# The skip term of a state-space scan written into the PSUM bank by ACT, the gate moved to DVE, and FFN weights binarised on ACT alone

## The chip, the cores and the metric

The kernel runs on one NeuronCore of a Trainium2 chip. A core has five engines that run side by side, each through its own list of instructions in order: PE (TensorE, matrix products), ACT (ScalarE, one input and a function), DVE (VectorE, element-wise work and scans), POOL (GpSimd, element-wise work) and SP (SyncE, which here only issues DMAs). They wait for each other through semaphores. The metric is the device time of one execution in microseconds (us); lower is better. All data is fp32.

## The reference

One layer of a network on x of shape 8 x 384 x 1024 (batch, channels, tokens). Its first half is a selective state-space model, its second half a feed-forward network (FFN) with binarised weights.

```python
t = layernorm(layernorm_over_channels(x))
xm, z = split(t @ in_proj_w.T)                  # 768 channels each
xc = silu(conv3(xm) + conv_b)
dt, Bm, Cm = split(xc @ x_proj_w.T)             # 24, 16, 16
dt = softplus(dt @ dt_proj_w.T + dt_proj_b)
dA  = exp(dt * A)                               # 16 states per channel
dBu = dt * xc * Bm
h_t = dA_t * h_{t-1} + dBu_t                    # along the 1024 tokens
y = (sum over states of h * Cm) + xc * D        # the skip term is xc * D
y = y * silu(z)                                 # the gate
x = x + gelu((y @ out_proj_w.T) @ mlp_w1.T + mlp_b1) @ mlp_w2.T + mlp_b2
...
# FFN, for each of 5 groups of rows of W1 (1536 x 384) and W2 (384 x 1536):
wg = W[g]; z = wg - wg.mean(); Wb[g] = z + (sign(z) - z)   # rows beyond 5 groups stay 0
y = x @ Wb.T + b; y = clip(y * 128 / (max|y| + eps), ...)
```

The FFN's quantisation works in 5 groups over the batch of 8, so that only the first five batch elements have an FFN output that is not zero.

## The kernel before

The work of each batch element b is cut into a front (`s1`: norms, input projection, convolution, dt), a scan (`s2`, `scan`, `scan_tile`), a back (`s3`: output projection and MLP) and, for b under 5, the FFN (`ffn`). Results pass between these parts through DRAM tensors. Once, at b = 0, `binarise` turns W1 and W2 into signs and stores them.

The scan of one batch element has 12 units. A unit (loop over m in `scan`) is one PSUM bank py of 128 x 512, the sum over states for its channels. It needs 8 scan tiles of 128 x 1024 (4 groups of states times 2 groups of channels). For each tile, `scan_tile` has ACT write da = Exp(dt * A) (L792), POOL write u = dtx * B (L797), DVE run the recurrence (L801), and then DVE (L818) or, for three of the eight, POOL (L815) multiply by C. After each four tiles PE adds the 16 results into py with 128 x 32 matmuls (L728); the first of them opens an accumulation group (`start=True`) and so overwrites the bank. Batch elements 0 and 7 are scanned as two halves of 512 tokens, with the state kept between them.

When a unit's sums are complete, xc and silu(z) for it are loaded into xr and zr. DVE computes xr = xr * D + py (L758), POOL multiplies xr by zr (L768, or L764 for the last batch element, straight into yg), and SP stores xr to the DRAM tensor yg_d (L774), from which the back loads it.

No order is written out by hand. `Plan.add` records each operation with an engine, a cost in microseconds and the tiles that it reads and writes. `Plan.run` then goes through them as a list scheduler: at each step the engine that can start first takes its most urgent operation that is ready by these costs, and the order in which that happens becomes the order of that engine's instructions. Scan work ranks first, and the sums (lane -1) before it. Buffers are rings: one each of xr, zr and y (the PSUM bank py), two of da, nine of u, three of mm (the PSUM banks for the projections). Where the plan sees PE idle for more than 0.7 us, it puts in spare matmuls (L376) of no use to the result. The costs are the functions at the top of the file, such as

```python
def c_act(n):
    return 0.22 + n * 0.00084
```

or numbers at the call. They say nothing to the chip; they set the order alone.

`binarise` passes over the weights twice. In the second pass it has, for each of six pieces of 1520 to 1536 elements a partition, POOL subtract the group's mean (L959), ACT take the Sign into another tile (L965), and POOL form sign - w (L970) and w + that (L974).

Of the kernel before, what the change touches and what calls it, by code (L numbers as in the profile page):

```python
# [26 lines left out]
F32 = mybir.dt.float32  # L27
AF = mybir.ActivationFunctionType
# [55 lines left out]
def c_act(n):  # L84
    return 0.22 + n * 0.00084


def c_dve(n):
    return 0.14 + n * 0.00105


def c_pool(n):
    return 0.13 + n * 0.0022

# [225 lines left out]
class Layer:  # L320
    def __init__(self, ctx, tc, a, out):
# [51 lines left out]
        self.constants()  # L373

        self.plan.spare = self.piece("mm", [P, T], "spare")
        self.plan.fill = lambda: self.nc.tensor.matmul(  # L376
# [91 lines left out]
    def norm(self, t, eps, scale):  # L468
# [45 lines left out]

        add("PE", MM, spread, r=[rstd], w=[p_r])
        add("DVE", c_dve(KC * T), lambda: nc.vector.tensor_mul(  # L516
# [5 lines left out]
    def s1(self, b):  # L522
# [47 lines left out]
        for half, cols in enumerate(HALVES):  # L570
# [4 lines left out]
            for m in range(KD):  # L575
                w = self.weights(r_w, KC, a["in_proj_w"][m])
                pm = self.mm3(w, t, [t[k] for k in range(KC)], [xc], "p_in")
                tap = [self.conv_w[:, m, j : j + 1] for j in range(3)]
                self.act(
                    lambda m=m, xc=xc: xc.real[:, m, :], lambda pm=pm: pm.real, AF.Identity,  # L580
                    c_act(T), r=[pm], w=[xc[m]], bias=self.conv_b[:, m : m + 1], scale=tap[2],
                )
                if half == 0:
                    add("ACT", 0.24, lambda m=m, pm=pm: nc.scalar.copy(  # L584
                        halo.real[:, m, :], pm.real[:, T - 2 :]
                    ), r=[pm], w=[halo[m]])
                for s in (1, 2):
                    add("DVE", c_dve(T) + 0.06, lambda m=m, xc=xc, pm=pm, s=s, tap=tap: (
                        nc.vector.scalar_tensor_tensor(  # L589
                            xc.real[:, m, s:], pm.real[:, : T - s], tap[2 - s],  # L590
                            xc.real[:, m, s:], ALU.mult, ALU.add,
                        )
                    ), r=[pm], w=[xc[m]])
            if half:
                def edge(xc=xc):
                    tmp = self.edge
                    for s in (1, 2):
                        tp = tmp[:, :, :s]
                        w = self.conv_w[:, :, 2 - s : 3 - s].to_broadcast([P, KD, s])
                        nc.gpsimd.tensor_mul(tp, halo.real[:, :, 2 - s :], w)  # L600
                        nc.gpsimd.tensor_add(xc.real[:, :, :s], xc.real[:, :, :s], tp)

                add("POOL", 0.7, edge, r=[halo[m] for m in range(KD)],
                    w=[xc[m] for m in range(KD)])
# [17 lines left out]
            for k in range(KD):  # L622
                if k % KC == 0:
                    w = self.weights(r_w, KC, a["dt_proj_w"][k // KC])
                i = k % DTC * DQ
                pd = self.piece("mm", [P, T], "p_dt")
                add("PE", MM / 2, lambda i=i, k=k, pd=pd, dbc=dbc, w=w: nc.tensor.matmul(  # L627
                    pd.real, w.real[i : i + R, k % KC, :], dbc.real[i : i + R, :],
# [38 lines left out]
    def scan(self, b, half, state):  # L667
# [30 lines left out]
        for m in range(DI // per_unit):  # L698
            py = self.piece("y", [P, T], "py")
            tiles = [range((2 * m + i) * wide, (2 * m + i + 1) * wide) for i in both]  # L700
            dts = [rep("dt", js) for js in tiles]
            dtxs = [rep("dtx", js) for js in tiles]
            batch = []
            for q in range(NQUAD):
# [13 lines left out]
                def sums(py=py, batch=batch):  # L718
                    for q, hcs in batch:
# [7 lines left out]
                        for p0, hc in parts:  # L727
                            nc.tensor.matmul(  # L728
                                py.real[p0 : p0 + DQ, :], self.fold, hc,
                                start=(q == 0), stop=(q == NQUAD - 1),  # L730
                            )
# [5 lines left out]

            def rows_of(name, half=half, m=m):

                if half is None:  # L740
                    return [(slice(0, P), m, slice(0, P))]
                mine = slice(half * DP, (half + 1) * DP)
                return [(slice(i * DP, (i + 1) * DP), 2 * m + i, mine) for i in both]

            def unit(name):
                r = self.piece(f"{name[0]}r", [P, T], f"{name[0]}r")
                d = self.dram[name, b]
                keys = [(h, i) for h in halves for i in both]
                for at, pair, its in rows_of(name):
                    self.plan.add("SP", 0.35, lambda at=at, pair=pair, its=its: (  # L750
                        nc.sync.dma_start(r.real[at, :], d.real[pair, its, :])
                    ), r=[d[k] for k in keys], w=[r], size=4 * P * n // wide)
                return r

            xr, zr = unit("xc"), unit("z")
            skip = self.d_pair if half is None else self.d_unit
            add("DVE", c_dve(T), lambda m=m, xr=xr, py=py, skip=skip: (
                nc.vector.scalar_tensor_tensor(  # L758
                    xr.real, xr.real, skip[:, m : m + 1], py.real, ALU.mult, ALU.add
                )  # L760
            ), r=[py], w=[xr])
            if b == B - 1:
                yg = self.last_yg[half]
                add("POOL", c_pool(T), lambda m=m, xr=xr, zr=zr, yg=yg: nc.gpsimd.tensor_mul(  # L764
                    yg.real[:, m, :], xr.real, zr.real
                ), r=[xr, zr], w=[yg[m]])
                continue
            add("POOL", c_pool(T), lambda xr=xr, zr=zr: nc.gpsimd.tensor_mul(  # L768
                xr.real, xr.real, zr.real
            ), r=[zr], w=[xr])  # L770
            d = self.dram["yg", b]
            for at, pair, its in rows_of("yg"):
                self.plan.add("SP", 0.35, lambda at=at, pair=pair, its=its, xr=xr: (
                    nc.sync.dma_start(d.real[pair, its, :], xr.real[at, :])  # L774
                ), r=[xr], w=[d[h, pair] for h in halves], size=4 * P * n // wide)

# [4 lines left out]
    def scan_tile(self, hcs, cols, n, dt_r, dtx_r, bq, cq, state, half, on_pool):  # L781
# [18 lines left out]
        for k, col in enumerate(cols):  # L800
            add("DVE", 0.13 + n * 0.0021, lambda k=k, col=col: nc.vector.tensor_tensor_scan(  # L801
                to.real[:, k, :], da.real[:, k, :], u.real[:, k, :],
                state.real[:, col : col + 1] if half else 0.0, ALU.mult, ALU.add,
            ), r=[da, u] + ([state[cols[0]]] if half else []), w=[to])
        if half == 0:
            c0, step = cols[0], cols[1] - cols[0]
            kept, last = lambda: state.real[:, c0 : c0 + step + 1 : step], n - 1
            if on_pool:
                add("POOL", 0.12, lambda: nc.gpsimd.tensor_copy(kept(), to.real[:, :, last]),
                    r=[to], w=[state[c0]])  # L810
            else:
                add("ACT", 0.25, lambda: nc.scalar.copy(kept(), to.real[:, :, last]),
                    r=[to], w=[state[c0]])
# [87 lines left out]
    def binarise(self, name, kt, n_out):  # L901
# [48 lines left out]
        for ks, ms in pieces:  # L950
            w = loaded(ks, ms)
            m0, n = ms.start, min(ms.stop, used) - ms.start

            def centre(w=w, m0=m0, n=n):
                for g in range(NUM_GROUPS):
                    lo, hi = max(g * gs - m0, 0), min((g + 1) * gs - m0, n)
                    if lo < hi:
                        wg = w.real[:, :, lo:hi]
                        nc.gpsimd.tensor_scalar(  # L959
                            wg, wg, 1.0, mean.real[:, g : g + 1], ALU.mult, ALU.add  # L960
                        )

            add("POOL", 1.8, centre, r=[mean], w=[w])
            sgn = self.piece("hid", [P, ks.stop - ks.start, ms.stop - ms.start], "sgn")
            self.act(lambda sgn=sgn, n=n: sgn.real[:, :, :n], lambda w=w, n=n: w.real[:, :, :n],  # L965
                     AF.Sign, c_act(KC * T), r=[w], w=[sgn])

            def less(w=w, sgn=sgn, n=n):
                wu, su = w.real[:, :, :n], sgn.real[:, :, :n]
                nc.gpsimd.tensor_sub(su, su, wu)  # L970

            def plus(w=w, sgn=sgn, m0=m0, n=n):
                wu, su = w.real[:, :, :n], sgn.real[:, :, :n]
                nc.gpsimd.tensor_add(wu, wu, su)  # L974
                if m0 + n == used < n_out:
                    nc.gpsimd.memset(w.real[:, :, n:], 0.0)

            add("POOL", c_pool(KC * T), less, r=[w], w=[sgn])
            add("POOL", c_pool(KC * T), plus, r=[sgn], w=[w])
            for m in range(ms.start // P, ms.stop // P):  # L980
# [40 lines left out]
    def ffn(self, b):  # L1021
# [14 lines left out]
        for m in range(KH):  # L1036
            w = self.weights("w_b", KC, w_d.real[m], r=[w_d[p] for p in need if p[1] == m])
            for h, cols in enumerate(HALVES):
# [6 lines left out]
                k = 2 * m + h  # L1045
                add("DVE", c_dve(T), lambda y=y, k=k: nc.vector.tensor_reduce(
                    mx.real[:, k : k + 1], y.real, AX.X, ALU.max, apply_absolute_value=True
# [7 lines left out]
        for h, cols in enumerate(HALVES):  # L1055
# [14 lines left out]
            for m in range(KC):  # L1070
# [8 lines left out]
                k = 2 * m + h  # L1079
                add("DVE", c_dve(T), lambda m=m, yh=yh, k=k: nc.vector.tensor_reduce(  # L1080
                    mx2.real[:, k : k + 1], yh.real[:, m, :], AX.X, ALU.max,
# [113 lines left out]
```

## Time and profile before

| | |
|---|---|
| Time, median of 3 runs | 3365.72 us (3360.21 to 3366.96) |
| Span of the profiled execution | 3369.4 us |
| Instructions in the profile | 32362 |
| DMA | 751.77 MB, 223 GB/s on average |
| Spare matmuls (L376) | 85.3 us of PE, 160 matmuls |
| First and last sums into py (L728) | 149.3 and 3281.8 us |

An fp32 matmul leaves two records in the profile, so that its counts are about twice the number of instructions. Busy time of an engine is the time in which it has an instruction under way; the lists of waits give, for idle time of an engine, what ended it. Costs of the plan and times of the profile are two different things: only the second are measured.

### The profile page before, as it was taken

To read this page: it belongs to the slowest core of one execution; us is meant where nothing else is said; L and a number is where in the kernel's file an instruction comes from. 1 tells how busy PE (TensorE), PEld (TensorE's weight loads), DVE (VectorE), ACT (ScalarE), POOL (GpSimd) and SP (SyncE) were. 2 spreads that over 40 slices of the span, in tenths; PEclk is the share of its full clock that TensorE was granted. 3 is DMA by queue.
4 is the path that set the end of the run, shared out by engine and by line. 5 is a ranking of instruction groups with operands and counts; after the bars stand their busy time and mean duration, and the time that the engine had idled before them with its cause. 6 is when DMAs were issued, how large, how long until landed. Compare 5 with 4: busy or idle time off the path is not lost.

```text
span 3369.4 us, 32362 instructions
## 1 busy us (share of the span) xinstructions
PE 3203.1 (95%) x10298; PEld 1327.3 (39%) x10298; DVE 2758.5 (82%) x2083; ACT 2005.1 (60%) x2212; POOL 2863.5 (85%) x1420
## 2 busy tenths in 40 slices
PE   8888799999989999899999999998999999999999
PEld 4333333344334344343444334433343444443334
DVE  3587588899978989878999888889996999888880
ACT  4777577656574557565565656565666455555551
POOL 1798787897989998799989799989999899999970
PEclk9988898999989999999999999999999999999999
DMA  6887877865788756886668667786678666766542
GB/s 189 286 252 234 234 228 234 284 202 177 232 264 260 234 190 219 252 270 217 205 208 279 219 211 256 267 255 196 217 237 293 208 193 211 238 200 191 175 131 76
DMA packets 369370, 751.77 MB, mean 223 GB/s; under 512 B 35376, under 2 KB 112688, under 8 KB 369200
## 3 DMA queue, kind: packets, MB, share of 16 engines
q1 hardware_dynamic: 367472, 749.60, 69.7%
q8 instruction: 83, 1.36, 0.2%
q14 instruction: 87, 0.71, 0.1%
q10 hardware_dynamic: 1728, 0.09, 0.0%
HBM read 569.21 MB, written 180.36 MB: 222 GB/s over the span
## 4 chain that ended last, share of the span: by engine, by line
PE 67%; DMA 11%; DVE 7%; ACT 6%; POOL 4%; issue 3%; SPq 1%; DVEq 0%; POOLq 0%; ACTq 0%
PE p_y L446 15%; PE p_o L446 13%; PE p_h L446 11%; PE py L728 8%; PE p_out L446 5%; PE p_z L446 5%; PE p_in L446 4%; DVE da L801 4%; DMA w_f<-in_in_proj_w 3%; ACT da L462 2%; DMA w_b<-in_mlp_w 2%; ACT L462 1%; PE p_dt L627 1%; PE p_sum L475 1%; POOL u L797 1%
## 5 line engine op out<-in xcount | busy, mean ns | idle before, releaser
L797 POOL TENSOR_TENSOR u<-dtx_r,bc 128x1024 f32<-128x1024 f32 x768 | 1790.0, 2361 | 100.7 <-DMA dtx_r<-dtx_d 68.0
L462 ACT ACTIVATE da<-dt_r,a_neg 128x1024 f32<-128x1024 f32 (+1 forms) x960 | 903.7, 946 | 617.2 <-DVE u L818 454.2
L801 DVE TENSOR_TENSOR_SCAN da<-da,u 128x1024 f32<-128x1024 f32 (+1 forms) x480 | 970.3, 2021 | 195.1 <-POOL u L797 111.3
L815 POOL TENSOR_TENSOR u<-u,bc 128x1024 f32<-128x1024 f32 x288 | 678.8, 2364 | 162.5 <-DVE u L801 145.7
L801 DVE TENSOR_TENSOR_SCAN u<-da,u 128x1024 f32<-128x1024 f32 (+1 forms) x288 | 572.6, 2010 | 68.1 <-ACT da L462 37.6
L818 DVE TENSOR_TENSOR u<-da,bc 128x1024 f32<-128x1024 f32 x480 | 586.3, 1221 | 12.2
L446 PE MATMUL p_h<-t,w_b 128*128 128x512 f32 x1152 | 517.6, 602 | 17.1 <-DMA w_b<-in_mlp_w 9.8
L446 PE MATMUL p_o<-g,w 128*128 128x512 f32 x1152 | 508.8, 597 | 2.5 <-DMA w<-in_mlp_w 2.4
L728 PE MATMUL py<-u,fold 128*32 128x512 f32 x3072 | 388.9, 615 | 19.3 <-DVE u L818 9.9
L446 PEld LDWEIGHTS p_h<-t,w_b 128*128 128x128 f32 x1152 | 216.6, 192 | 309.0 <-issue 263.7
L446 PEld LDWEIGHTS p_o<-g,w 128*128 128x128 f32 x1152 | 216.0, 190 | 293.8 <-issue 279.4
L446 PE MATMUL p_y<-tn,w_b 128*128 128x512 f32 x720 | 329.1, 602 | 0.3 <-DVE tn L516 0.2
L446 PE MATMUL p_y<-gf,w_n 128*128 128x512 f32 x720 | 320.1, 600 | 7.4 <-ACT gf L462 4.1
L462 ACT ACT_TABLE_LOAD x218 | 279.7, 1283 | 14.4 <-DMA dt_r<-dt_d 6.5
L446 PE MATMUL p_out<-yg,w 128*128 128x512 f32 x552 | 249.7, 604 | 13.2 <-DMA yg<-yg_d 11.3
L446 PE MATMUL p_in<-t,w_f 128*128 128x512 f32 x504 | 235.6, 615 | 22.2 <-DMA w_f<-in_in_proj_w 9.0
L446 PE MATMUL p_z<-t,w_f 128*128 128x512 f32 x504 | 231.4, 607 | 16.3 <-DMA w_f<-in_in_proj_w 11.7
L446 PEld LDWEIGHTS p_y<-gf,w_n 128*128 128x128 f32 x720 | 135.7, 192 | 190.6 <-issue 168.4
L446 PEld LDWEIGHTS p_y<-tn,w_b 128*128 128x128 f32 x720 | 135.6, 192 | 181.5 <-issue 162.5
L462 ACT ACTIVATE g<-p_h,v_mlp_b 128x512 f32<-128x512 f32 x192 | 128.0, 679 | 118.2 <-PE p_h L446 118.0
L728 PEld LDWEIGHTS py<-u,fold 128*32 128x32 f32 x3072 | 82.4, 110 | 290.0 <-issue 207.4
L589 DVE SCALAR_TENSOR_TENSOR xc<-p_in,conv_w,xc 128x511 f32<-128x511 f32 x192 | 141.7, 743 | 66.8 <-ACT halo L584 39.9
(100 smaller groups left out, 2776.8 us busy)
## 6 DMA issues: line engine op xcount, KB each, us to landing
dtx_r<-dtx_d SPq DMA_DIRECT2D x144, 512.0 KB, 5.3
dt_r<-dt_d SPq DMA_DIRECT2D x144, 512.0 KB, 5.4
w_b<-in_mlp_w SPq DMA_DIRECT2D x192, 192.0 KB, 2.9
w<-in_mlp_w SPq DMA_DIRECT2D x96, 384.0 KB, 4.0
w_f<-in_in_proj_w SPq DMA_DIRECT2D x168, 192.0 KB, 4.5
y_d<-y SPq DMA_DIRECT2D x120, 256.0 KB, 4.2
gf<-y_d SPq DMA_DIRECT2D x20, 1536.0 KB, 9.3
xc_d<-xc SPq DMA_DIRECT2D x32, 768.0 KB, 8.8
```

Source lines behind the costliest of these rows:

```text
L446: self.nc.tensor.matmul(p.real, w.real[:, w0 + k, :], t.real[:, k0 + k, :], start=start and k == 0, stop=stop and k == n - 1,)
L462: lambda: self.nc.scalar.activation(out(), in_(), func, **{k: v() if callable(v) else v for k, v in kw.items()}),
L475: nc.tensor.matmul(p_sum.real, self.ones, t.real[:, k, :], start=(k == 0), stop=(k == KC - 1))
L589: nc.vector.scalar_tensor_tensor(xc.real[:, m, s:], pm.real[:, : T - s], tap[2 - s], xc.real[:, m, s:], ALU.mult, ALU.add,)
L627: add("PE", MM / 2, lambda i=i, k=k, pd=pd, dbc=dbc, w=w: nc.tensor.matmul(pd.real, w.real[i : i + R, k % KC, :], dbc.real[i : i + R, :], ...
L728: nc.tensor.matmul(py.real[p0 : p0 + DQ, :], self.fold, hc, start=(q == 0), stop=(q == NQUAD - 1),)
L797: add("POOL", 2.36, lambda: nc.gpsimd.tensor_mul(u.real, dtx_r.real, spread(bq)), r=[dtx_r, bq], w=[u])
L801: add("DVE", 0.13 + n * 0.0021, lambda k=k, col=col: nc.vector.tensor_tensor_scan(to.real[:, k, :], da.real[:, k, :], u.real[:, k, :], sta ...
L815: add("POOL", 2.36, lambda: nc.gpsimd.tensor_mul(u.real, u.real, spread(cq)), r=[cq], w=[u])
L818: add("DVE", 1.21, lambda: nc.vector.tensor_mul(u.real, da.real, spread(cq)), r=[da, cq], w=[u])
```

## The change

In `scan`, xr is loaded ahead of the unit's scan tiles, and ACT writes the skip term xr * D into the bank py. PE's sums are then added onto it: none of them opens an accumulation group any more. So that this adds from the start, one matmul ("first") writes the whole bank at the beginning of the kernel. When the sums are complete, DVE multiplies py by zr, into zr (or into yg for the last batch element), and zr is stored. DVE's scalar-tensor-tensor and POOL's multiply are gone.

In `binarise`, ACT takes Sign(w + (-mean)) in place, one instruction for each group within a piece; POOL's subtraction of the mean and its two further passes are gone, and the second tile with them.

Several costs of the plan are changed too.

```diff
 def c_act(n):
-    return 0.22 + n * 0.00084
+    return 0.25 + n * 0.00084
 def c_dve(n):
-    return 0.14 + n * 0.00105
+    return 0.19 + n * 0.00102
 def c_pool(n):
-    return 0.13 + n * 0.0022
+    return 0.18 + n * 0.00214
...
+        first = psum.tile([P, T], F32, tag="y", name="first", bufs=1)
+        self.nc.tensor.matmul(
+            first, self.ones, self.one.to_broadcast([P, T]), start=True, stop=True
+        )
...
-        add("PE", MM, spread, r=[rstd], w=[p_r])
+        add("PE", 1.25, spread, r=[rstd], w=[p_r])
...
-                    c_act(T), r=[pm], w=[xc[m]], bias=self.conv_b[:, m : m + 1], scale=tap[2],
+                    c_act(T) + 0.1, r=[pm], w=[xc[m]], bias=self.conv_b[:, m : m + 1], scale=tap[2],
...
-                    add("ACT", 0.24, lambda m=m, pm=pm: nc.scalar.copy(
+                    add("ACT", 0.16, lambda m=m, pm=pm: nc.scalar.copy(
...
-                add("POOL", 0.7, edge, r=[halo[m] for m in range(KD)],
+                add("POOL", 1.5, edge, r=[halo[m] for m in range(KD)],
...
-                add("PE", MM / 2, lambda i=i, k=k, pd=pd, dbc=dbc, w=w: nc.tensor.matmul(
+                add("PE", 1.0, lambda i=i, k=k, pd=pd, dbc=dbc, w=w: nc.tensor.matmul(
...
             tiles = [range((2 * m + i) * wide, (2 * m + i + 1) * wide) for i in both]
...
+            skip = self.d_pair if half is None else self.d_unit
+            xr = unit("xc")
+            self.act(lambda py=py: py.real, lambda xr=xr: xr.real, AF.Identity, c_act(T),
+                     r=[xr], w=[py], scale=skip[:, m : m + 1])
             dts = [rep("dt", js) for js in tiles]
...
-                                start=(q == 0), stop=(q == NQUAD - 1),
+                                start=False, stop=(q == NQUAD - 1), skip_group_check=True,
...
-            xr, zr = unit("xc"), unit("z")
-            skip = self.d_pair if half is None else self.d_unit
-            add("DVE", c_dve(T), lambda m=m, xr=xr, py=py, skip=skip: (
-                nc.vector.scalar_tensor_tensor(
-                    xr.real, xr.real, skip[:, m : m + 1], py.real, ALU.mult, ALU.add
-                )
-            ), r=[py], w=[xr])
+            zr = unit("z")
             if b == B - 1:
                 yg = self.last_yg[half]
-                add("POOL", c_pool(T), lambda m=m, xr=xr, zr=zr, yg=yg: nc.gpsimd.tensor_mul(
-                    yg.real[:, m, :], xr.real, zr.real
-                ), r=[xr, zr], w=[yg[m]])
+                add("DVE", c_dve(T), lambda m=m, py=py, zr=zr, yg=yg: nc.vector.tensor_mul(
+                    yg.real[:, m, :], py.real, zr.real
+                ), r=[py, zr], w=[yg[m]])
                 continue
-            add("POOL", c_pool(T), lambda xr=xr, zr=zr: nc.gpsimd.tensor_mul(
-                xr.real, xr.real, zr.real
-            ), r=[zr], w=[xr])
+            add("DVE", c_dve(T), lambda py=py, zr=zr: nc.vector.tensor_mul(
+                zr.real, py.real, zr.real
+            ), r=[py], w=[zr])
...
-                    nc.sync.dma_start(d.real[pair, its, :], xr.real[at, :])
-                ), r=[xr], w=[d[h, pair] for h in halves], size=4 * P * n // wide)
+                    nc.sync.dma_start(d.real[pair, its, :], zr.real[at, :])
+                ), r=[zr], w=[d[h, pair] for h in halves], size=4 * P * n // wide)
...
-            add("DVE", 0.13 + n * 0.0021, lambda k=k, col=col: nc.vector.tensor_tensor_scan(
+            add("DVE", (0.2 if half else 0.15) + n * 0.00209, lambda k=k, col=col: nc.vector.tensor_tensor_scan(
...
-                add("POOL", 0.12, lambda: nc.gpsimd.tensor_copy(kept(), to.real[:, :, last]),
+                add("POOL", 0.2, lambda: nc.gpsimd.tensor_copy(kept(), to.real[:, :, last]),
...
-                add("ACT", 0.25, lambda: nc.scalar.copy(kept(), to.real[:, :, last]),
+                add("ACT", 0.16, lambda: nc.scalar.copy(kept(), to.real[:, :, last]),
...
-                        nc.gpsimd.tensor_scalar(
-                            wg, wg, 1.0, mean.real[:, g : g + 1], ALU.mult, ALU.add
-                        )
-
-            add("POOL", 1.8, centre, r=[mean], w=[w])
-            sgn = self.piece("hid", [P, ks.stop - ks.start, ms.stop - ms.start], "sgn")
-            self.act(lambda sgn=sgn, n=n: sgn.real[:, :, :n], lambda w=w, n=n: w.real[:, :, :n],
-                     AF.Sign, c_act(KC * T), r=[w], w=[sgn])
...
-            add("POOL", c_pool(KC * T), less, r=[w], w=[sgn])
-            add("POOL", c_pool(KC * T), plus, r=[sgn], w=[w])
+                        nc.scalar.activation(wg, wg, AF.Sign, bias=mean.real[:, g : g + 1])
+
+            add("ACT", c_act(KC * T) + 0.6, sign, r=[mean], w=[w])
+            if m0 + n == used < n_out:
+                add("POOL", 0.12, lambda w=w, n=n: nc.gpsimd.memset(w.real[:, :, n:], 0.0), w=[w])
...
-                add("DVE", c_dve(T), lambda y=y, k=k: nc.vector.tensor_reduce(
+                add("DVE", 0.67, lambda y=y, k=k: nc.vector.tensor_reduce(
...
-                add("DVE", c_dve(T), lambda m=m, yh=yh, k=k: nc.vector.tensor_reduce(
+                add("DVE", 0.67, lambda m=m, yh=yh, k=k: nc.vector.tensor_reduce(
```

More of the change, by code (lines that the diff above doesn't have):

```diff
@@ L700, in scan, with rows_of, unit @@
             tiles = [range((2 * m + i) * wide, (2 * m + i + 1) * wide) for i in both]
+            def rows_of(m=m):
+                if half is None:
+                    return [(slice(0, P), m, slice(0, P))]
+                mine = slice(half * DP, (half + 1) * DP)
+                return [(slice(i * DP, (i + 1) * DP), 2 * m + i, mine) for i in both]
+            def unit(name):
+                r = self.piece(f"{name[0]}r", [P, T], f"{name[0]}r")
+                d = self.dram[name, b]
+                keys = [(h, i) for h in halves for i in both]
+                for at, pair, its in rows_of():
+                    self.plan.add("SP", 0.35, lambda at=at, pair=pair, its=its: (
+                        nc.sync.dma_start(r.real[at, :], d.real[pair, its, :])
+                    ), r=[d[k] for k in keys], w=[r], size=4 * P * n // wide)
+                return r
+            skip = self.d_pair if half is None else self.d_unit
+            xr = unit("xc")
+            self.act(lambda py=py: py.real, lambda xr=xr: xr.real, AF.Identity, c_act(T),
+                     r=[xr], w=[py], scale=skip[:, m : m + 1])
             dts = [rep("dt", js) for js in tiles]
@@ L736, in scan @@
                 batch = []
[L738 to L753, printed above, removed]
@@ L767, in scan @@
                 continue
-            add("POOL", c_pool(T), lambda xr=xr, zr=zr: nc.gpsimd.tensor_mul(
-                xr.real, xr.real, zr.real
-            ), r=[zr], w=[xr])
+            add("DVE", c_dve(T), lambda py=py, zr=zr: nc.vector.tensor_mul(
+                zr.real, py.real, zr.real
+            ), r=[py], w=[zr])
             d = self.dram["yg", b]
-            for at, pair, its in rows_of("yg"):
-                self.plan.add("SP", 0.35, lambda at=at, pair=pair, its=its, xr=xr: (
-                    nc.sync.dma_start(d.real[pair, its, :], xr.real[at, :])
-                ), r=[xr], w=[d[h, pair] for h in halves], size=4 * P * n // wide)
+            for at, pair, its in rows_of():
+                self.plan.add("SP", 0.35, lambda at=at, pair=pair, its=its, zr=zr: (
+                    nc.sync.dma_start(d.real[pair, its, :], zr.real[at, :])
+                ), r=[zr], w=[d[h, pair] for h in halves], size=4 * P * n // wide)
@@ L952, in binarise, with sign @@
             m0, n = ms.start, min(ms.stop, used) - ms.start
-            def centre(w=w, m0=m0, n=n):
+            def sign(w=w, m0=m0, n=n):
                 for g in range(NUM_GROUPS):
@@ L958, in centre @@
                         wg = w.real[:, :, lo:hi]
-                        nc.gpsimd.tensor_scalar(
-                            wg, wg, 1.0, mean.real[:, g : g + 1], ALU.mult, ALU.add
-                        )
-            add("POOL", 1.8, centre, r=[mean], w=[w])
-            sgn = self.piece("hid", [P, ks.stop - ks.start, ms.stop - ms.start], "sgn")
-            self.act(lambda sgn=sgn, n=n: sgn.real[:, :, :n], lambda w=w, n=n: w.real[:, :, :n],
-                     AF.Sign, c_act(KC * T), r=[w], w=[sgn])
[L968 to L976, printed above, removed]
-            add("POOL", c_pool(KC * T), less, r=[w], w=[sgn])
-            add("POOL", c_pool(KC * T), plus, r=[sgn], w=[w])
+                        nc.scalar.activation(wg, wg, AF.Sign, bias=mean.real[:, g : g + 1])
+            add("ACT", c_act(KC * T) + 0.6, sign, r=[mean], w=[w])
+            if m0 + n == used < n_out:
+                add("POOL", 0.12, lambda w=w, n=n: nc.gpsimd.memset(w.real[:, :, n:], 0.0), w=[w])
             for m in range(ms.start // P, ms.stop // P):
```

## The prediction

> **What bounds the kernel now.** I read the page first: busy shares, then the chain of waits.
>
> ```profile
> PE 3203.1 (95%) x10298; PEld 1327.3 (39%) x10298; DVE 2758.5 (82%) x2083; ACT 2005.1 (60%) x2212; POOL 2863.5 (85%) x1420
> ...
> PE 67%; DMA 11%; DVE 7%; ACT 6%; POOL 4%; issue 3%; SPq 1%; DVEq 0%; POOLq 0%; ACTq 0%
> ```
>
> PE is busy 95% and carries 67% of the chain, so the end is set by PE's work plus whatever PE loses. Next, the windows, cut at the gates (L758) of scan units 28, 84 and 96 of 96, to see where it loses.
>
> ```profile
> 0.00:1135.00 1135.00, 1028.32 (x3302) 426.05 (x3303) 875.96 (x710) 733.24 (x856) 917.13 (x495) 0.93 0.76 237
> 1135.00:2914.00 1779.00, 1736.17 (x5722) 723.59 (x5721) 1564.18 (x1091) 1042.87 (x1038) 1618.81 (x760) 0.99 0.71 231
> 2914.00:3282.00 368.00, 355.22 (x1082) 140.88 (x1080) 314.63 (x279) 212.38 (x301) 326.30 (x166) 0.99 0.57 176
> 3282.00:3369.40 87.40, 83.40 (x198) 36.77 (x194) 3.75 (x5) 16.59 (x18) 1.26 (x1) 0.99 0.24 77
> ```
>
> After the length of the stage the columns are PE, PEld, DVE, ACT and POOL busy, granted clock, DMA share and GB/s. PE idles 107 us in the first stage (clock 0.93), 43 in the middle, 13 in the third and 4 in the last, where nothing but PE still works. In the middle PE is 98% busy, POOL 91%, DVE 88%: three engines near their limit. The waits show how they couple.
>
> ```profile
> ACT da L462 <- DVE u L818: 454.2, 226, 5.8
> ...
> POOL u L815 <- DVE u L801: 145.7, 56, 13.6
> ...
> DVE da L801 <- POOL u L797: 113.6, 30, 10.0
> ...
> DVE u L801 <- POOL u L797: 46.4, 12, 9.6
> ...
> DVE xr L758 <- PE py L728: 43.6, 27, 5.2
> ```
>
> DVE waits 160 us for POOL's product u; ACT mostly waits for DVE, so ACT has room. SyncE's queue also waits 170.8 us (51 waits) for POOL's gate before it can store it (L774).
>
> **The Trainium skill.** "PSUM — Partial Sum Buffer", Specifications: GpSimd can neither read nor write PSUM, ScalarE and VectorE can. The trace agrees: no POOL row touches py, so POOL's gate needs DVE's copy in xr first. The same page, The four PSUM rules: only TensorE changes the has-written bits, and a matmul that does not begin a group adds where the bit is set; hence the one matmul "first". No row of before tests that. "ScalarE: Activation LUTs", What ACT_TABLE_LOAD costs: 186 ns + 0.833 ns per element + 93 ns per pointer operand, so an estimate of 705 ns for 512 elements and one pointer; Exp of that form measures 691. "Perfetto Trace Analysis", Identifying the Most-Contended Engine: matmul busy time does not measure nearness to the limit. So I count PE's work separately below.
>
> **The change part by part.** Durations come from these groups.
>
> ```profile
> L768 POOL TENSOR_TENSOR xr<-xr,zr 128x512 f32<-128x512 f32 x84 | 107.0, 1274 | 5.9 <-DVE xr L758 5.9
> ...
> L462 ACT ACTIVATE xc<-p_in,v_conv_b,conv_w 128x512 f32<-128x512 f32 x96 | 73.7, 773 | 98.8 <-PE p_in L446 98.8
> ...
> L758 DVE SCALAR_TENSOR_TENSOR xr<-xr,v_D_pair,py 128x512 f32<-128x512 f32 x72 | 53.0, 736 | 31.0 <-PE py L728 27.7 <-DMA yg<-yg_d 3.0
> ...
> L516 DVE TENSOR_TENSOR t<-t,p_r 128x1536 f32<-128x1536 f32 x16 | 27.9, 1745 | 27.9 <-PE p_r L511 27.9
> L480 DVE SCALAR_TENSOR_TENSOR t<-p_sum,t 128x1536 f32<-128x1536 f32 x16 | 27.9, 1744 | 13.0 <-PE p_sum L475 13.0
> ```
>
> *POOL* loses 96 gates (84 L768 + 12 L764, 107.0 + 15.3 = 122 us) and the binarising: L959 about 13, L970 and L974 six each at 3.42 = 41. Together 177 us, 6% of its 2863; 90 of them before unit 28 (28 x 1.27 + 54).
>
> *DVE* swaps 96 scalar-tensor-tensors of 0.736 us for 96 multiplies with one PSUM input. L516 and L480 show both forms at equal size: 1745 and 1744 ns. Net 0; bounds -10 (at the 0.64 that the quickest L758 took) and +2.
>
> *ACT* gains 96 skip writes to PSUM, a form no row shows: 0.69 (Exp, one pointer) to 0.77 (L462 xc, two); I take 0.70 = 67 us. Sign goes from 6 pieces to 22 with the same elements: 16 more fixed parts of about 0.27 (Exp: 1116 ns at 1024, 691 at 512) = 4. Sum 71 on an engine 60% busy, hidden in the 454 us in which it waits for DVE. Bounds 0 and, if each skip write made Exp and so DVE late by its own length, 67.
>
> *Waits.* The skip write waits for the last unit's gate (one bank) and for xr; PE's first sums of a unit wait for it. In the built order it stands behind about 4 of the unit's 8 Exps, and the sums need 4 finished tiles; the da buffers keep ACT only about two tiles ahead of DVE. So it usually comes in time. Behind it stand Exps, and DVE waits for those. The gate stands 2 to 3 scans into the next unit, as L758 did. Cost taken 5 us; bounds 0 and 96 x 1 = 96.
>
> *DMA.* The same 96 gate stores, from zr; SyncE's wait falls at least by POOL's 1.27 us per gate. xr's load moves ahead of dt_r and dtx_r in program order and no longer waits for a store; zr's does. Both need one landing (3.2 us median) in a unit of 31 us (1779 / 56): nothing.
>
> *PE.* One matmul more (0.86) and 17 spare fills more (177 for 160, at 85.3 / 160 = 0.53: 9 us).
>
> *The planner's costs* now lie nearer the trace: p_dt 0.43 to 1.0 (measured about 0.85), a 512-wide ACT evacuation 0.65 to 0.68 (0.68). They reorder every queue; no single row prices that.
>
> *PE's ledger.* From the chain, in the tail:
>
> ```profile
> 3303.60 30.90 PE p_h L446 x72
> ```
>
> An fp32 matmul leaves two records, so these are 36 matmuls at 0.858. Counting every PE instruction so gives 2976 us; 85 spares, 166 idle, and 142 left for slow clock and narrow tiles make 3369. In the built order PE has 82 us of work behind the last sums of before, 188 in the changed one. Work and last gate: before 2893 by 3282 us; after 2789.
>
> I take from idle: a quarter of the first stage (-27), as POOL there drops a tenth and frees W1, W2 and the first scans; a fifth of the middle (-9); 9 of the third, since a backlog now fills it. From slow clock in the first stage 5. Against: 9 + 1 + 5. Sum -35: 3334 of the profile's 3369. The runs' median lies 4 lower than the profile: **3330**.
>
> Check: 82 us of work took 87 after the last gate, so 188 take about 197, and the gate must come at 3137. DVE's 2754 us by then are 87.8%, against 83.9% before and 87.9% in the middle stage; POOL falls from 87% to 86%. Possible, not generous.
>
> **The rivals.** *A, a larger gain.* DVE loses all its 169 us of waits for POOL (with 9 for L815), and 35 of those for PE, which has 104 us less to do by then. Gate at 3078, end 3275, runs 3271. For it: POOL's relief equals the wait. Against: POOL waits 146 us for DVE too.
>
> *B, slower.* DVE becomes the bound. PE takes its work in the order laid down, and that order now supposes a scan that runs ahead; DVE lost no work. If POOL's relief takes only 60 us from DVE's waits, the gate comes at 3222, 197 follow: 3419, runs 3415. The point where it decides: last gate later than 3172, 110 us gained. For it: DVE reaches 95% only in the best of windows of 100 us; against: DVE's waits for POOL alone are 169.
>
> *C, nothing.* The relief only moves idle time to POOL, and PE's losses stay: 3366. For it: PE 98% busy in the middle; against: the first stage.
>
> **How the numbers follow.** Forecast 0.50, own range 3300 to 3355; A 0.18; B 0.22; C 0.10. Faster 0.68, same 0.10, slower 0.22, with 0.2% (7 us) as what can be told from no change. The range reaches to A and, with the unknown costs (67 and 96), towards B: 3255 to 3405.
>
> **What would show it.** POOL near 2686 busy, DVE near 2758, ACT near 2076; DVE's wait for POOL well under 160; last gate near 3137 and about 197 us behind it; PE's idle in the first 1135 us near 80. Wrong if the gate is later than 3172, or if ACT's waits for the gate show up as DVE's waits for da above today's 129.

## The result, and the profile after

The changed kernel takes 3415.89 us (median; 3408.64 to 3419.28), the kernel before 3366.34 beside it: a ratio of 1.0145, 95% interval 1.012 to 1.017. It is slower by about 50 us, where the forecast was 3330 and faster. The profiled execution spans 3417.5 us, 48.1 more than before's.

The page of the changed kernel, busy time and chain of waits:

```profile
PE 3218.3 (94%) x10334; PEld 1330.1 (39%) x10334; DVE 2749.1 (80%) x2083; ACT 2067.6 (61%) x2323; POOL 2692.3 (79%) x1290
...
PE 10%; DMA 0%; SPq 0%; DVE 0%; issue 0%
```

POOL has 171 us less to do, ACT 63 more, DVE 9 less: the parts came out close to their prices. The chain is followed back over a tenth of the span only, so that its shares can't be set against those of before. PE is busy 15 us longer than before and idle 33 longer (3417.5 - 3218.3 = 199 against 166), which is the whole loss. Of the 15, spare matmuls are 3.5 (88.8 against 85.3); the rest was not traced.

Windows of the changed kernel, cut at the gates (now L771 and L767) of units 28, 84 and 96, with the columns of before (length, PE, PEld, DVE, ACT, POOL busy, clock, DMA share, GB/s):

```profile
0.00:1107.15 1107.15, 1011.77 (x3321) 424.09 (x3322) 873.45 (x709) 737.12 (x882) 826.24 (x429) 0.95 0.75 237
1107.15:2850.30 1743.15, 1655.77 (x5445) 672.37 (x5446) 1552.98 (x1083) 1074.10 (x1099) 1549.49 (x709) 0.97 0.71 230
2850.30:3224.23 373.93, 361.84 (x1129) 149.93 (x1130) 315.25 (x282) 220.85 (x307) 316.52 (x154) 0.99 0.60 188
3224.23:3417.50 193.27, 188.97 (x442) 83.72 (x442) 7.45 (x10) 35.56 (x37) 0.00 (x0) 1.00 0.28 88
```

The last gate comes at 3224 instead of 3282, 58 us sooner. Behind it PE still works for 193 us, where it was 87: 106 more. 106 - 58 = 48, the difference of the spans. And PE, which ends up with that backlog, idles 87 us in the middle stage (1743.15 - 1655.77), twice the 43 of before. The chain of waits of the changed kernel, in order of time (start, length, what), shows what lies behind the last sums:

```profile
3222.31 1.85 PE py L754 x16
3224.16 2.77 PE p_h L450 x6
3226.93 30.90 PE p_o L450 x72
3257.83 15.45 PE p_out L450 x36
3273.28 0.43 PE spare L380 x2
3273.72 30.90 PE p_h L450 x72
3304.62 30.90 PE p_o L450 x72
3335.52 15.45 PE p_out L450 x36
...
3351.40 30.90 PE p_h L450 x72
3382.30 30.91 PE p_o L450 x72
```

These are the backs of both halves of the last batch element, and the rest of one before; in the kernel before only the second half's was left. PE runs through them without a gap: nothing else is needed any more.

The list of waits of the changed kernel (in total, times, longest):

```profile
POOL u L818 <- DVE u L804: 227.7, 71, 20.0
...
DVE da L804 <- ACT da L466: 100.7, 41, 5.9
DVE u L804 <- ACT da L466: 85.1, 32, 8.3
DVE zr L771 <- PE py L754: 47.3, 22, 6.9
...
DVE da L804 <- POOL u L800: 37.5, 15, 6.1
...
ACT py L466 <- DVE zr L771: 33.3, 25, 2.8
...
DVE u L804 <- POOL u L800: 19.2, 8, 7.3
```

DVE's wait for POOL's u falls from 160 to 57 us, as hoped; as much as half of that comes back as a wait for ACT's da (186 against 129). POOL waits longer for DVE (228 against 146). A new wait appears on ACT: 33 us before the skip write. PE's own idle time behind ACT goes from 54 to 105 us, summed over the list. The groups of the new instructions:

```profile
L771 DVE TENSOR_TENSOR zr<-py,zr 128x512 f32<-128x512 f32 x84 | 57.0, 678 | 47.5 <-PE py L754 47.3
...
L466 ACT ACTIVATE py<-xr,v_D_pair 128x512 f32<-128x512 f32 x72 | 49.1, 681 | 35.7 <-DVE zr L771 30.5 <-DMA mid_d<-res 4.9
```

This suggests two causes: skip writes that hold up ACT, or the order, which leaves more behind the last gate.

### The profile page after: what moved, and what is told of

The parts are those of the page before. It is cut to its first block, busy times and chain, and to the rows that moved or that the text cites. A ratio compares the mean times of both kernels' runs of the same rounds, so it can differ in the third digit from the quotient of the medians.

```text
span 3417.5 us, 32462 instructions
## 1 busy us (share of the span) xinstructions
PE 3218.3 (94%) x10334; PEld 1330.1 (39%) x10334; DVE 2749.1 (80%) x2083; ACT 2067.6 (61%) x2323; POOL 2692.3 (79%) x1290
## 5 line engine op out<-in xcount | busy, mean ns | idle before, releaser
L450 PE MATMUL p_y<-gf,w_n 128*128 128x512 f32 x720 | 329.9, 614 | 33.1 <-ACT dt L466 11.6
```

Of the source, the lines that this page charges most:

```text
L450: self.nc.tensor.matmul(p.real, w.real[:, w0 + k, :], t.real[:, k0 + k, :], start=start and k == 0, stop=stop and k == n - 1,)
```

## The experiments

Theory A puts the loss down to ACT: the skip writes and their waits. Theory O puts it down to the order in which the plan lays out the queues. "The plan's own end", which some expectations name, is the time at which `Plan.run` itself, with its own costs, sees the last operation end; it comes out when the kernel is built and is no time of the chip.

### Parts alone

**POOL's relief in the old order.** 84 of POOL's 96 gates (L768) and its two further passes over the weights (L970, L974) emit nothing; the plan still counts them, so that all queues keep the order of before. The 12 gates of the last batch element and the subtraction of the mean stay.

```diff
-            add("POOL", c_pool(T), lambda xr=xr, zr=zr: nc.gpsimd.tensor_mul(
-                xr.real, xr.real, zr.real
-            ), r=[zr], w=[xr])
+            add("POOL", c_pool(T), lambda xr=xr, zr=zr: None, r=[zr], w=[xr])
...
-                nc.gpsimd.tensor_sub(su, su, wu)
...
-                nc.gpsimd.tensor_add(wu, wu, su)
...
```

> The kernel before with every queue in its old order and 82 us of PE work behind the last gate; POOL's gate (L768, 84 of 96) and the passes L970 and L974 are left out, so the gate of seven batch elements and the sign of the weights are missing from the result. POOL has 148 us less to do. Theory O (the order decides: POOL's relief brings the last gate forward by about 58 us as in the changed kernel, and the time is the last gate plus PE's work behind it): gate near 3230, time 3305 to 3330. Theory A (the skip writes and waits on ACT cost the changed kernel its time): the same here, since ACT gets nothing; a time under 3340. Rival N (POOL's relief is worth nothing): 3355 to 3370.

Measured: 3352.62 us, a ratio of 0.9967 (0.9955 to 0.9979). Its page:

```profile
PE 3192.8 (95%) x10298; PEld 1323.4 (40%) x10298; DVE 2759.5 (83%) x2083; ACT 2005.5 (60%) x2212; POOL 2723.2 (81%) x1324
```

POOL is 140 us less busy, and 13 us come of it. The last gate comes at 3258, not at 3230. Both theories expected more than this: in an order laid out for a POOL that is not relieved, the relief is worth little.

**The costs alone.** The kernel before, with only the numbers of the plan changed, such as:

```diff
-        add("PE", MM, spread, r=[rstd], w=[p_r])
+        add("PE", 1.25, spread, r=[rstd], w=[p_r])
...
-                add("PE", MM / 2, lambda i=i, k=k, pd=pd, dbc=dbc, w=w: nc.tensor.matmul(
+                add("PE", 1.0, lambda i=i, k=k, pd=pd, dbc=dbc, w=w: nc.tensor.matmul(
...
```

> The kernel before with the plan's new costs alone; same operations, another order, 131 us of PE work behind the last gate. Theory O: POOL is not relieved, so the gate stays near 3280 and 131 us follow: about 3415, most of the loss. Theory A: no skip writes, so no loss: 3355 to 3375.

Measured: 3444.34 us, ratio 1.0243 (1.0217 to 1.027): slower than the changed kernel itself, by the order alone. The page (span 3433.1 us):

```profile
PE 3222.8 (94%) x10334; PEld 1335.5 (39%) x10334; DVE 2758.3 (80%) x2083; ACT 2003.2 (58%) x2208; POOL 2864.2 (83%) x1420
```

DVE, ACT and POOL do what they did before; PE idles 210 us. The gate comes at 3297, and 136 us follow. Theory O had 3415 and missed by 29, with a gate that it left near 3280; theory A had no loss.

**The flow alone.** The skip term, gate and binarising of the changed kernel, with the costs of before:

```diff
 def c_act(n):
-    return 0.25 + n * 0.00084
+    return 0.22 + n * 0.00084
...
-        add("PE", 1.25, spread, r=[rstd], w=[p_r])
+        add("PE", MM, spread, r=[rstd], w=[p_r])
...
```

> The skip term, gate and binarising of the changed kernel with the old costs of the plan; 165 us of PE work behind the last gate. Theory O: gate 3220 plus about 173: 3390 to 3400, less of a loss than the changed kernel. Theory A: the full loss remains, 3405 to 3425, since the costs of the plan do nothing to the chip.

Measured: 3377.49 us, ratio 1.0033 (1.0016 to 1.0049). Less of a loss than either theory had; the gate comes at 3211 and 170 us follow.

**The skip writes left out** of the changed kernel, in its order. The first of PE's sums opens a group again, so that the bank starts afresh without them:

```diff
-            self.act(lambda py=py: py.real, lambda xr=xr: xr.real, AF.Identity, c_act(T),
-                     r=[xr], w=[py], scale=skip[:, m : m + 1])
+            add("ACT", c_act(T), lambda py=py: None, r=[xr], w=[py])
...
-                                start=False, stop=(q == NQUAD - 1), skip_group_check=True,
+                                start=(q == 0), stop=(q == NQUAD - 1),
```

> The changed kernel with every queue in its order and 188 us of PE work behind the last gate, with the 96 skip writes left out (the skip term is missing from the result) and the sums opening their group again. Theory A: PE's idle time behind ACT falls from 105 to about 55 us and the time by about 45, to 3365 to 3380. Theory O: ACT's 66 us lay beside other work; 3405 to 3417.

Measured: 3414.56 us, against 3415.89 with them. The page (span 3412.1 us):

```profile
PE 3215.6 (94%) x10334; PEld 1329.9 (39%) x10334; DVE 2750.4 (81%) x2083; ACT 2009.0 (59%) x2227; POOL 2693.2 (79%) x1290
```

ACT is 59 us less busy, and PE idles 196 us instead of 199. Theory A falls: the skip writes and their 33 us of waiting lie beside other work. PE's idle time behind ACT, which theory A had at 55 us, is still 95 of the 105, and DVE's wait for da is still 185: both waits are there without the skip writes.

**POOL's work put back** into the changed kernel, in its order: a multiply by one of each gated tile, ahead of the store (and likewise of yg for the last batch element).

```diff
-            add("DVE", c_dve(T), lambda py=py, zr=zr: nc.vector.tensor_mul(
-                zr.real, py.real, zr.real
-            ), r=[py], w=[zr])
+            add("DVE", c_dve(T), lambda py=py, zr=zr: (
+                nc.vector.tensor_mul(zr.real, py.real, zr.real),
+                nc.gpsimd.tensor_mul(zr.real, zr.real, self.one.to_broadcast([P, T])),
+            ), r=[py], w=[zr])
...
```

> The changed kernel, every queue in its order, with a POOL multiply by one of each gated tile (96 of 128x512) put back between DVE's gate and the store: the result is the same. If POOL's relief is worth what it was in the old order (13 us for 148 us of POOL work): 3425 to 3432. If it is worth the 58 us by which the last gate came sooner: 3465 to 3480. If nothing: 3410 to 3420.

Measured: 3465.26 us, ratio 1.0299 (1.0257 to 1.0341), 49 us above the changed kernel. The group of the added multiplies, and the windows cut at the last gate:

```profile
L776 POOL TENSOR_TENSOR zr<-zr,one 128x512 f32<-128x512 f32 x84 | 87.6, 1043 | 31.7 <-DVE zr L775 31.1 <-DMA w_f<-in_in_proj_w 0.2
...
0.00:3252.57 3252.57, 3032.59 (x9893) 1247.59 (x9894) 2743.12 (x2074) 2032.18 (x2286) 2788.19 (x1385) 0.97 0.71 226
3252.57:3445.50 192.93, 188.97 (x442) 83.70 (x442) 7.45 (x10) 35.58 (x37) 1.04 (x1) 1.00 0.29 88
```

About 100 us of POOL (with 12.5 for the last batch element) and the later stores cost 49 here, where taking 140 away gained 13 in the old order. The gate comes at 3253, 28 us later, with the same 193 behind it; this profile is of the fastest of the four runs, 3447. So the changed kernel's order depends on the relief, and something larger than it goes the other way. How much of the 49 is POOL's work, and how much the multiply's place between gate and store, was not separated.

### Drawing the order anew

The plan decides by small differences. If one nanosecond in one fixed cost is enough to change what follows, each kernel's time is a draw among many orders. Three nudges of the kernel before:

```diff
-    return 0.22 + n * 0.00084
+    return 0.221 + n * 0.00084
```

> The kernel before with one cost of the plan moved by one nanosecond (ACT's fixed part 0.22 to 0.221); same operations, another order from PE's 480th instruction on, 82 us of PE work behind the last gate. Theory L (luck: the order of the kernel before is a good draw among many, and any change of the costs draws anew): 3375 to 3435. Theory D (directed: it is the direction of the new costs that loses): within 10 us of 3366. Theory T (the work behind the last gate sets the time): 3366, as its 82 us are those of before.

```diff
-    return 0.14 + n * 0.00105
+    return 0.141 + n * 0.00105
```

> The kernel before with DVE's fixed part of the plan moved by one nanosecond (0.14 to 0.141); 146 us of PE work behind the last gate. Theory L: 3375 to 3435. Theory D: within 10 us of 3366. Theory T: some 60 us more than before, about 3425.

```diff
-    return 0.13 + n * 0.0022
+    return 0.131 + n * 0.0022
```

> The kernel before with POOL's fixed part of the plan moved by one nanosecond (0.13 to 0.131); 124 us of PE work behind the last gate. Theory L: 3375 to 3435. Theory D: within 10 us of 3366. Theory T: some 40 us more than before, about 3405.

and one of the changed kernel:

```diff
-    return 0.19 + n * 0.00102
+    return 0.191 + n * 0.00102
```

> The changed kernel with DVE's fixed part of the plan moved by one nanosecond (0.19 to 0.191); 170 us of PE work behind the last gate. Theory L: a new draw, anywhere from 3365 to 3435, on average below the draws of the kernel before by what POOL's relief is worth (13 us in the old order). Theory D: within 10 us of 3416. Theory T: 18 us less than the changed kernel, about 3398.

Measured: 3364.67 (ratio 0.9996), 3436.61 (1.0211, 1.0186 to 1.0237) and 3395.89 (1.0083) for the kernel before; 3433.55 for the changed one. One nanosecond in DVE's cost loses 70 us with the same operations. Theory D is refuted by that, as it had every nudge within 10 us of 3366. Theory L, which had 3375 to 3435 for all three, holds for one, and misses the others by 10 and 2. The windows of that run, cut at its last gate:

```profile
0.00:3289.49 3289.49, 3073.78 (x9949) 1265.21 (x9950) 2752.48 (x2077) 1968.16 (x2173) 2864.32 (x1419) 0.96 0.70 225
3289.49:3440.30 150.81, 146.91 (x344) 65.13 (x344) 5.25 (x7) 32.03 (x35) 1.26 (x1) 1.00 0.28 85
```

The gate is 7 us later than before's, and 151 us follow it instead of 87; PE idles 216 us up to it. More idle PE before the gate and a longer tail behind it are what the changed kernel shows too; here they come without its change. Theory T hit the three nudges of before within 12 us, and missed after_dve_1ns by 36, as theory O, which reckons with the same tail, had missed costs_alone: the gate moves with the draw too.

Theory P was then formed from these runs: the plan's own end, plus what the chip adds. Three draws that were chosen for an early end of the plan, one each for three sets of operations and costs:

```diff
 # the changed kernel
-    return 0.19 + n * 0.00102
+    return 0.186 + n * 0.00102
...
-    return 0.18 + n * 0.00214
+    return 0.182 + n * 0.00214
```

> The changed kernel with DVE's fixed cost in the plan 4 ns lower and POOL's 2 ns higher; the same operations and 142 us of PE work behind the last gate. The end that the plan itself reckons is 3293, against 3364 for the changed kernel and 3272 for the kernel before. Theory P (the time is the plan's own end, which any nudge of a cost draws anew, plus 50 to 105 us that the chip adds): 3293 plus 66, the mean of the two changed kernels run so far: 3359, within 3345 to 3375, so the loss of the change is gone. Theory D (the new costs are worse by their direction): 3400 or more.

```diff
 # the kernel before; its fixed costs to 0.216, 0.142 and 0.132 as well
-IDLE = 0.7
+IDLE = 1.0
...
-FRONTS = 3
+FRONTS = 4
...
-SLACK = 1.4
+SLACK = 1.0
```

> The kernel before with fixed costs moved by 4, 2 and 2 ns and three thresholds of the plan (SLACK 1.0, FRONTS 4, IDLE 1.0); the same operations, 82 us behind the last gate. The plan's own end is 3253, 19 below the kernel before. Theory P: 3335 to 3360. Theory T (only the work behind the last gate counts): 3366 as before. Theory L in its strong form (before is already the best draw): 3366 or more.

```diff
 # the flow alone; its fixed costs to 0.222, 0.142 and 0.133 as well
-EARLY = 2
+EARLY = 1
...
-SLACK = 1.4
+SLACK = 1.6
```

> The changed flow with the old costs moved by 2, 2 and 3 ns and two thresholds of the plan (SLACK 1.6, EARLY 1); 121 us behind the last gate. The plan's own end is 3261. Theory P: 3261 plus the 77 of the flow run so far, 3339, within 3325 to 3355, which would be below both kernels. Theory T: gate 3215 plus 125: 3340. Theory A (skip writes on ACT cost time) or D: 3366 or more.

Measured: 3357.20 for the changed kernel (ratio 0.9976, 0.9964 to 0.9988), 3373.70 for the kernel before (1.0023, 1.0011 to 1.0036) and 3354.69 for the flow (0.9973, 0.9959 to 0.9988). The first is the answer to the question of the case: the changed kernel, with the same operations and with two costs moved by 4 and 2 ns, is 59 us faster than the changed kernel, and a little faster than the kernel before. Its windows:

```profile
0.00:3202.93 3202.93, 3030.77 (x9875) 1241.88 (x9876) 2745.04 (x2076) 2047.47 (x2298) 2694.36 (x1290) 0.97 0.73 231
3202.93:3349.50 146.57, 142.63 (x334) 63.24 (x334) 5.20 (x7) 32.02 (x35) 0.00 (x0) 0.99 0.29 88
```

The busy times of DVE, ACT and POOL are those of the changed kernel within 12 us; PE has 45 us less (3173.4 against 3218.3), with fewer spare matmuls, and the tail is 147 instead of 193. Theory P missed the second of these runs by 14 us: its own end, 3253, is the earliest of all, and the chip adds 121.

To see whether the operations or the costs lose on average, blind nudges of one nanosecond completed the sets:

```diff
 # the flow alone: ACT's, DVE's and POOL's fixed part, one at a time
-    return 0.22 + n * 0.00084
+    return 0.221 + n * 0.00084
```

> The changed flow with the old costs, ACT's fixed part one nanosecond higher, a nudge taken blindly; 136 us of PE work behind the last gate, the plan's own end 3265. Theory P (the plan's end plus about 80): 3335 to 3365. Theory L with an average gain of the operations: below 3388, the mean of the kernel before's draws.

> The changed flow with the old costs, DVE's fixed part one nanosecond higher, taken blindly; 196 us of PE work behind the last gate, the plan's own end 3323. Theory P: 3390 to 3420, a loss against the kernel before from the same operations that gain in another draw. Theory D (the old costs are good ones): under 3380.

> The changed flow with the old costs, POOL's fixed part one nanosecond higher, taken blindly; 136 us of PE work behind the last gate, the plan's own end 3278. Theory P: 3345 to 3375. Theory D: the same.

```diff
 # the changed kernel: ACT's and POOL's fixed part, one at a time
-    return 0.25 + n * 0.00084
+    return 0.251 + n * 0.00084
```

> The changed kernel, ACT's fixed part one nanosecond higher, taken blindly; 150 us of PE work behind the last gate, the plan's own end 3321. Theory P (the plan's end plus 52 to 79 for the changed kernel's draws): 3373 to 3400. Theory D (the new costs lose by their direction): 3405 or more.

> The changed kernel, POOL's fixed part one nanosecond higher, taken blindly; 131 us of PE work behind the last gate, the plan's own end 3307. Theory P: 3359 to 3386. Theory D (the new costs lose by their direction): 3405 or more.

```diff
 # the costs alone: DVE's fixed part
-    return 0.19 + n * 0.00102
+    return 0.191 + n * 0.00102
```

> The kernel before with the plan's new costs, DVE's fixed part one nanosecond higher, taken blindly; 88 us of PE work behind the last gate, the plan's own end 3326. Theory P: 3326 plus the 85 of the first run with the costs alone: 3400 to 3420. Theory D: near that run's 3444.

Measured, in the order above: 3358.31, 3398.72, 3376.54; 3377.62, 3365.89; 3401.90. Theory P holds them all within 2 us of its ranges; theory D had 3405 or more for the changed kernel, and falls. Together, with the unnudged kernel first in each row:

| Operations, costs | Times, us | Mean |
|---|---|---|
| before, old costs | 3366, 3365, 3437, 3396 | 3391 |
| changed, old costs | 3377, 3358, 3399, 3377 | 3378 |
| before, new costs | 3444, 3402 | 3423 |
| changed, new costs | 3416, 3434, 3378, 3366 | 3398 |

Within a row of four the times spread over 40 to 72 us; between the first two rows lie 13, between the second and the fourth 20. A mean of four has an uncertainty of half its row's standard deviation, 8 to 17 us here, so that a difference between two of them is uncertain by 18 or 19. Whether the operations gain some 13 us on average, and whether the new costs lose some 20, is therefore not settled. That the verdict on the pair at hand, +50 us, is within the spread of a row is settled. It sets a lucky draw against an unlucky one: of the five draws of the kernel before, chosen one included, it is within 2 us of the quickest, and of the five of the changed kernel only one is slower.

The last gate and what follows it, from the profiled executions of all draws:

| | Last gate, us | Behind it, us |
|---|---|---|
| before, old costs (5) | 3270 to 3289, mean 3279 | 86 to 151, mean 108 |
| changed, old or new costs (10) | 3203 to 3257, mean 3224 | 126 to 201, mean 159 |

The change does bring the scan's end forward, by 55 us on average. But PE then has 51 us more of its work left. PE's idle time, out of which a gain would mostly have to come, is 182 us on average in the first row and 178 in the second. I read this so, though no run tests it by itself: PE is the bound; what POOL is spared lets the scan run ahead of PE, and what PE doesn't do alongside the scan it does behind it.

The waits that a single pair of traces shows are in part the draw too. All of DVE's waits for u are 169 us before and 63 after; but in before_act_1ns, with the work and the time of before (3364.67), they are 121. Over the draws of this table they fall from 130 to 60 on average.

The plan's own end against the measured time, over the 17 kernels whose plan and operations agree: the chip adds 83 us on average, with a standard deviation of 18, and the two correlate at 0.85. It was 3272 for the kernel before and 3364 for the changed one: each plan reckons with its own costs, but that the new order ends later could be read there before any run.

## Why the prediction was wrong

*The prices of the operations* held. POOL lost 171 us (177 forecast), ACT gained 63 (71), a skip write took 0.681 us (0.70, from Exp; the 705 ns that I estimated from the Trainium skill, "ScalarE: Activation LUTs", What ACT_TABLE_LOAD costs, is 24 ns high). DVE's gate took 0.678 where I had put 0.736, so that DVE gained 5.6 us where I counted nothing.

*The waits* held in their worth, not in their place. Skip write and waits together cost nothing that can be measured (3415.89 with them, 3414.56 without; 5 forecast). What stands behind a waiting skip write is not Exps alone but the evictions of PE's results too, which I didn't name; leaving the writes out shows that it didn't matter. The sign that I had named for it, DVE's waits for da above 129, came (186) and misled: they are 185 with the writes left out, and 168 already in before_act_1ns.

*The planner's costs* are the step that failed. "They reorder every queue; no single row prices that" was followed by a price of zero and no width at all. The runs put on it: +78 us for the costs alone, and up to 72 us between orders that differ by one nanosecond in one cost; another order of the same changed operations takes 59 us less. That the new numbers lie nearer the trace was no reason for a better order.

*PE's ledger* failed by that. "I take from idle: a quarter of the first stage, a fifth of the middle, 9 of the third" supposed the old order with less to wait for. PE's idle time fell by 11 in the first stage (27 forecast) and rose by 45 in the middle (9 less forecast); in the third it fell by 1. Of the 45 in the middle, 37 are idle behind ACT (47 us against 10). They come with the order and not with the skip writes: with these left out PE still idles 46 us behind ACT in the same stretch, and 20 in after_other_draw. The order that I had counted, with 188 us behind the last sums, was right: they took 193 (197 forecast). What I did wrong was to count that tail as given and then to ask of the scan what it would need (a gate at 3137) instead of what POOL's relief could give. The gate came at 3224.

*Rival B* had the numbers: a gate at 3222, 197 us behind it, 3415. Its point of decision, a gate later than 3172, was the right reading. Its mechanism, DVE as the bound, is not what the runs show: DVE is busy 85% up to the gate (2742 of 3224), and the same DVE work ends at 3203 in another draw. So its 3415 beside the measured 3415.89 is luck. It was right about the order supposing a scan that runs ahead; that a new order is a new draw belongs to no rival, and was missing.

Why one order idles PE 220 us (before_dve_1ns) and another 159 (before_act_1ns) was not traced to single waits, nor were the waits behind ACT traced to what ACT does ahead of them; which orders are good can so far be told only from the plan's own end, roughly, and from a run.

## What to carry to other kernels

Where a list scheduler lays out the queues, a change of an operation and the change of order that comes with it are two effects: nudge a cost that means nothing, a few times on both sides, before crediting or blaming the operation. Read what is left on the bounding engine behind the last step of the other chain: here, relieving an engine that is not the bound brought that step forward by 55 us on average, and left 51 us more behind it. And a cost model made truer is not by itself a better order.

## What the runs showed of the hardware

DVE's multiply with one input in PSUM took 678 ns at 128x512, and the scalar-tensor-tensor with the same PSUM input 736, though at 128x1536 the two take 1745 and 1744. The pairs are not quite alike: at 1536 the PSUM input is one bank repeated three times, and the scalar is a constant, where at 512 it is a column of D; which of these makes the 58 ns is not shown. POOL's multiply by a broadcast single column took 1043 ns (pool_work_put_back), against 1274 with two full inputs of the same size (before).

That PE's sums add onto what ACT wrote into the bank is the design of the change. These runs don't show it: a time says nothing of what the bank holds.
